# Flamingo gated layer on one core: VectorE takes a share of the first quantisations, smaller first context loads, tiles 1 and 2 loaded early, a shorter LayerNorm chain

## The chip, the cores and the metric

The kernel runs on one core of one Trainium2 chip. The metric is device time in microseconds (us) of one execution, lower is better; the time of a kernel is the median over several executions. The profile is one further execution, recorded by the hardware.

## The reference

Inputs are tokens `x` [2, 1024, 2048] and a context `cx` [2, 2048, 2048], both f32. What is computed:

```
def fake_quant(x, s, z):                    # s, z: one number each
    return (clip(round(x / s + z), 0, 255) - z) * s

x = x + tanh(g_xattn) * (fake_quant(layernorm(x)) @ fake_quant(ctx))     # per batch, 1024x2048 @ 2048x2048
y = layernorm(x)
logits = y @ route_w.T                      # 8 experts, the best one is taken
h = y @ A.T                                 # 8 experts of rank 16
x = x + tanh(g_ffn) * ((one_hot(best) * best_logit * h) @ Bw)
```

The quantised numbers are integers of at most 8 bits, so the kernel holds them as f16 with the middle (128) taken off, multiplies those, and puts scale and zero points back with a row sum and a column sum.

## The kernel before

**Tiling.** The 2048 tokens are 16 tiles `t` of 128 rows (0 to 7 are batch 0, 8 to 15 batch 1). The context of a batch is four strips `s` of 512 columns; a strip has 16 blocks of 128 rows and is loaded in four pieces `q` of 1 MB (four blocks each). I number the pieces of batch 0 by `4 s + q`: pieces 0 to 3 are strip 0, 4 to 7 strip 1, and so on to 15.

**Work of a context piece** (`strip`): SP's queue loads it into a staging buffer `st` (four of them for batch 0), ScalarE scales, shifts and rounds it into int16 (`scale`, L429), VectorE clamps it at 255, takes 128 off and turns it into f16 (`clamp`, L436). The strip `q` is then the moving operand of the matmuls. Column sums `cs` come from 16 matmuls with ones (strip 0, L454) or from VectorE additions and one matmul (L465 to L470, L480), and ScalarE writes them to `corr` (L487).

**Work of a token tile** (`tokens`): load, mean and variance (by VectorE with bn_stats, L530 to L539, for tiles in STATV, otherwise by two ScalarE passes, L545 and L554), `pow` on GpSimd (L575), a chain of 128x1 operations on VectorE (`scale`, L566 to L571), quantisation on ScalarE (`quant`, L589), clamp on VectorE (L595), turning by 16 TensorE transposes (`pq`, L613) and two copies (L496) into `q1t`, or by a DMA transpose (tiles in TURN), and a row sum (L628 on VectorE for tiles in SUMV, L630 on ScalarE).

**Products** (`group`): for each tile and strip 16 matmuls (`mm`, L657) accumulate in one of four PSUM banks; VectorE adds the bank to `x` (L686), then row and column corrections (L691); tiles in LATE have the correction added first (L669) and need one operation per strip (L678). **The second half** (`ffn`): x is turned (TensorE `px` L775, or VectorE and DMA, `turned` and `across`, for tiles in MOVE), multiplied by `war` (`hl`, L757 and L781), the expert is picked on VectorE (L830 to L839), the result is turned (`pw`, `wht`), multiplied by `wb` (`po`, L864), added (L872) and stored.

**Order.** Nothing runs in a loop's order. Every piece of work is a task with an engine, an assumed cost and a rank; `Plan.walk` simulates the engines and gives each engine a fixed instruction order, which the hardware then follows strictly: an instruction that waits holds everything behind it on its engine. Ranks come from the tables CTX, LEAD, XLEAD, XL0, AFTER, SUM and COR. `sets` lists tiles that go through a strip together: tiles 0, 1, 2 share each strip, so TensorE has 3 x 16 matmuls for each strip that it is given.

In the order of before, the first matmul group is strip 1 of tile 0, and the pieces of strips 0 and 1 are loaded and quantised mixed (4, 5, 0, 6, 1, 7, 2, 3), with x of tile 3 loaded ahead of x of tile 2.

Of the kernel before, what the change touches and what calls it, by code (L numbers as in the profile page):

```python
# [9 lines left out]
F32 = mybir.dt.float32  # L10
# [146 lines left out]
def flamingo_gated_kernel(  # L157
# [112 lines left out]
    def gates():  # L270

        nc.vector.tensor_scalar(zm1, z1, MID, None, ALU.subtract)
        nc.vector.tensor_scalar(zm2, z2, MID, None, ALU.subtract)
        nc.vector.tensor_scalar(c, th[:, 0:1], s1, s2, ALU.mult, ALU.mult)
        nc.vector.tensor_scalar(cd1, zm1, c, -1.0, ALU.mult, ALU.mult)
        nc.vector.tensor_scalar(cd2, zm2, c, -1.0, ALU.mult, ALU.mult)
        nc.vector.tensor_scalar(ckd, cd1, zm2, -float(D), ALU.mult, ALU.mult)
# [3 lines left out]

    sets = [[0, 1, 2], [3], [4], [5, 6], [7], [8, 9]] + [[t] for t in range(10, NT)]
    groups = [(t, s) for tiles in sets for s in range(NN) for t in tiles]
# [10 lines left out]

    LATE = {4, 5, 6, 7, 14}
    STATV = {0, 1, 2, 5, 15}
    SUMV = {0, 2, 5, 6, 8, 14, 15}
    COPYV = {0, 1, 2, 4, 5, 7, 9, 12, 14}
    ONES = {0}
    SUM = [-1, 8.5, 0.5, 0.5, -1, 5.5, -1, 2.5, 5.5, 2.5, -1, 3.5, 5.5, 2.5, 0.5, 8.5]  # L300
    LEAD = [4, 4, 2, 8, 6, 3, 5, 14, 5, 8, 8, 12, 7, 7, 3, 14]
    XLEAD = [4, 4, 4, 4, 2, 1, 1, 4, 10, 6, 2, 1, 0, 1, 2, 2]
    XL0 = {0: -101, 1: -2.3, 2: 1.8, 3: -0.3}
    AFTER = [1.2, 4.2, 0.3, 3.2, 0.7, 0.7, 5.2, 3.2, 0.7, 0.7, 4.2, 6.2, 4.2, 2.2, 4.2, 3.2]
    CTX = [2, 6, 5, 4, 5, 4, 3, 3]
    COR = [7.5, 1.5, 1.5, 1.5, -0.5, 2.5, 2.5, 0.5]
    SLACK = 4.0
    VIA = {0, 1, 2, 3, 4, 5, 6, 8, 9, 10, 12}
    TWO = {1, 3, 5, 6, 9, 10, 11, 12, 13, 14}
    XL = {14, 15}  # L310
    SP, ACT, DVE, PE, POOL = "SP", "ACT", "DVE", "PE", "POOL"
    add = plan.add
# [15 lines left out]
    def spread(i, j, rank, needs):  # L328

        bc = buf("cs", f"bc{i}", [P, NC], F32)  # L330
        m = add(
            PE, 0.3, rank,
            lambda: nc.tensor.matmul(bc.ap()[:, : j - i], dmean[:1, :], row[:, i:j], start=True, stop=True),
            needs + [t_one], [bc],
        )

        def out():
            nc.vector.tensor_scalar(raw[:, i:j], bc.ap()[:, : j - i], float(D), None, ALU.mult)
            if i == 0:
                nc.vector.reciprocal(rs1, s1)  # L340
                nc.vector.reciprocal(rs2, s2)

        return add(DVE, 0.6, rank + 48, out, [m], [bc])

# [16 lines left out]
    )  # L361
    t_sc = add(DVE, 1.2, 0.5, gates, needs=[t_th, t_rs])

# [46 lines left out]
    def strip(b, s):  # L410
# [5 lines left out]
        for q in range(NQ):  # L416
            st = flat(f"st{b}", f"st_{b}_{s}_{q}", F32, D)
            rank = i - CTX[b * NN + s] + q * len(tiles) / NQ

            def load(q=q, st=st):  # L420
                rows = cx[b, q * QK * P : (q + 1) * QK * P, ts(s, NC)]
                nc.sync.dma_start(  # L422
                    st.ap().rearrange("p (k n) -> p k n", k=QK),
                    rows.rearrange("(k p) n -> p k n", p=P),
                )

            def scale(q=q, st=st):
                part = qb.ap()[:, ts(q, QK), :]
                nc.scalar.activation(  # L429
                    part.bitcast(I16), st.ap().rearrange("p (k n) -> p k n", k=QK), AF.Relu,  # L430
                    bias=z2, scale=rs2,
                )

            def clamp(q=q):
                part = qb.ap()[:, ts(q, QK), :]
                nc.vector.tensor_scalar(part, part.bitcast(I16), QMAX, MID, ALU.min, ALU.subtract)  # L436

            a = t_ctx[b, s, q] = add(
                SP, 0.5, rank, load, [t_ctx[0, NN - 1, NQ - 1]] if b else [], [st],
                nbytes=4 * P * QK * NC,  # L440
            )
            d = add(ACT, 2.12, rank, scale, [a, t_rs], [st, qb])
            parts.append(add(DVE, 0.7, rank, clamp, [d], [qb]))
        t_q2[b, s] = parts
# [3 lines left out]
        if b * NN + s in ONES:  # L448
            m = None
            for q in range(NQ):  # L450
# [6 lines left out]

                m = add(PE, 0.216 * QK, rank, sums, [parts[q], t_set] + ([m] if m else []), [cs, qb])
        else:
# [38 lines left out]
    def tokens(t):  # L498
# [4 lines left out]
        xb[t] = xx = buf("xl" if t in XL else "x", f"x_{t}", [P, D], F32)  # L503
        pieces = NN if early else 1
        w = D // pieces
        loads = []
        for i in range(pieces):
            loads.append(
                add(
                    ACT if i % 2 else SP, 0.5, XL0.get(t, rank - XLEAD[t]),  # L510
                    lambda i=i: (nc.scalar if i % 2 else nc.sync).dma_start(  # L511
                        xx.ap()[:, ts(i, w)], x[b, ts(m, P), ts(i, w)]
# [5 lines left out]
        qb = flat("half", f"q1_{t}", F16, D)  # L518
        mine = small.tile([P, 28], F32, name=f"mine_{t}")
        mv, wk, acc_sums[t], fs_[t], top_[t] = (  # L520
            mine[:, i:j] for i, j in ((0, 4), (4, 12), (12, 16), (16, 24), (24, 28))
        )
        y, u, v, a, nb, rw, r, ve = (wk[:, i : i + 1] for i in range(8))
        mean, var, nmean, ssum = (mv[:, i : i + 1] for i in range(4))
        if t in STATV:
# [10 lines left out]
            def variance():  # L536
                nc.vector.bn_aggr(mv[:, :2], bn.ap())
                nc.vector.tensor_scalar(ve, var, EPS, None, ALU.add)
                nc.vector.tensor_scalar(nmean, mean, -1.0, None, ALU.mult)  # L539

            ag = add(DVE, 0.6, rank, variance, stats, [bn])
        else:
# [7 lines left out]
                lambda: nc.vector.tensor_scalar(nmean, ssum, -1.0 / D, None, ALU.mult), [d],  # L550
            )
            d = add(
                ACT, 2.3, rank,
# [10 lines left out]
        def scale():  # L564

            nc.vector.tensor_scalar(u, ve, y, None, ALU.mult)  # L566
            nc.vector.scalar_tensor_tensor(v, u, -0.5, y, ALU.mult, ALU.mult)
            nc.vector.scalar_tensor_tensor(u, v, 1.5, y, ALU.add, ALU.mult)

            nc.vector.tensor_scalar(a, u, rs1, None, ALU.mult)  # L570
            nc.vector.scalar_tensor_tensor(nb, nmean, a, z1, ALU.mult, ALU.add)  # L571

        pw = add(
            POOL, 0.3, rank,
            lambda: nc.gpsimd.tensor_tensor(y, ve, mhalf, ALU.pow), [ag, t_set],  # L575
        )
        ts_ = add(DVE, 1.2, rank, scale, [pw, t_rs])
        if t == 0:
            t_sc.needs.append(ts_)
        q1t[t] = qt = buf("q1t", f"q1t_{t}", [P, KC, P], F16)  # L580
        H = 2 if early else 1
        hw = D // H
# [3 lines left out]
        for h in range(H):  # L586
# [9 lines left out]

            d = add(ACT, 2.1 / H, rank, quant, [ts_] + loads, [xx, qb])
            clamps.append(add(DVE, 0.7 / H, rank, clamp, [d], [qb]))
            t_read.setdefault(t, []).append(d)
# [48 lines left out]
    def group(t, s):  # L648
# [5 lines left out]
        for k in range(KC):  # L654
# [4 lines left out]
                ),  # L659
                [t_q2[b, s][k // QK], t_q1t[t][k // 8]] + ([p] if p else []), [acc, qt, qb],  # L660
            )
# [282 lines left out]
```

## Time and profile before

| | us |
|---|---|
| runs | 397.11, 401.61, 399.99: median 399.99 |
| the profiled execution | 396.57 |
| its span on the core | 394.7 |
| TensorE busy, as recorded | 375.0 (95%) |
| VectorE busy | 300.7 (76%) |
| ScalarE busy | 241.4 (61%) |
| granted TensorE clock | 0.993 |

The page divides the span into 40 slices, each 9.9 us; a digit is the busy share in tenths:

```profile
PE   6686999999999999999999999999999999999894
PEld 5433455658644464645765654444644655666571
DVE  4776988996985859778678679899688787676543
```

TensorE's row is below 9 in the first four slices and again in the second to last. In the first of these the core mostly waits for data; what each engine does there is seen in the timeline and in windows of 10 us.

### The profile page before, as it was taken

Reading aid. Unit: us, or ns where it says so; the run is one execution under the profiler, and the core shown is the slowest. Engines: PE = TensorE matmul, PEld = TensorE weight load, DVE = VectorE, ACT = ScalarE, POOL = GpSimd, SP = SyncE. Lnnn points to the kernel's source line nnn. Section 1 sums busy time; section 2 is a strip of 40 time slices with the busy share of each in tenths; the row PEclk is TensorE's granted clock in tenths of the full one; section 3 lists DMA queues with packets and bytes.
Section 4 is the critical chain, followed back from the end, with each engine's and each line's share of the span. In section 5 each row is a group of like instructions: output and inputs, shape, how many; then the busy total and the mean of one; then the engine's idle time right before and its main releaser. Section 6 shows DMA issues by size and latency. Waiting matters only on the chain.

```text
span 394.7 us, 5336 instructions
## 1 busy us (share of the span) xinstructions
PE 375.0 (95%) x1969; PEld 216.8 (55%) x1969; DVE 300.7 (76%) x711; ACT 241.4 (61%) x225; POOL 23.2 (6%) x52
## 2 busy tenths in 40 slices
PE   6686999999999999999999999999999999999894
PEld 5433455658644464645765654444644655666571
DVE  4776988996985859778678679899688787676543
ACT  2998998759424680897897995939846220422330
POOL 3000000010010100010001100101000000000000
PEclk9899999999999999999999999999999999999998
DMA  7999999411469728789687978667447557766405
GB/s 272 394 398 387 387 366 405 167 31 24 118 254 338 206 44 237 293 269 372 224 248 274 343 193 319 256 198 160 78 151 204 165 176 208 219 171 208 139 18 213
DMA packets 50018, 90.07 MB, mean 228 GB/s; under 512 B 21192, under 2 KB 23240, under 8 KB 45256
## 3 DMA queue, kind: packets, MB, share of 16 engines
q1 hardware_dynamic: 45172, 69.80, 54.4%
q0 software_dynamic: 2224, 15.73, 10.0%
q10 hardware_dynamic: 2596, 4.20, 4.4%
q8 instruction: 15, 0.25, 0.2%
q14 instruction: 11, 0.09, 0.1%
HBM read 58.79 MB, written 23.07 MB: 207 GB/s over the span
## 4 chain that ended last, share of the span: by engine, by line
PE 74%; DMA 16%; SPq 3%; ACT 2%; DVE 2%; ACTq 1%; issue 1%
PE mm L657 45%; PE po L864 11%; PE hl L781 7%; PE hl L757 6%; DMA st<-in_ctx_dram 5%; DMA across<-away 4%; DMA across<-turned 4%; PE px L775 3%; DMA away<-turned 3%; ACT turned L753 1%; SPq L422 1%; SPq L731 1%; ACTq L731 1%; PE pq L613 1%; SPq L511 1%; DMA x<-in_x_dram 1%
## 5 line engine op out<-in xcount | busy, mean ns | idle before, releaser
L657 PE MATMUL mm<-q,q1t 128*128 128x512 f16 x1024 | 234.6, 381 | 6.1 <-DVE q L436 3.4
L657 PEld LDWEIGHTS <-q1t 128*128 128x128 f16 x1024 | 100.3, 98 | 126.1 <-issue 16.8
L429 ACT ACTIVATE q<-st,raw,rs 128x2048 int16<-128x2048 f32 x32 | 66.4, 2090 | 14.4 <-PE mm L657 10.0
L872 DVE SCALAR_TENSOR_TENSOR x<-po,th,x 128x512 f32<-128x512 f32 x64 | 47.6, 750 | 22.7 <-PE po L864 19.8
L864 PE MATMUL po<-wb,wht 128*128 128x512 f32 x128 | 60.7, 595 | 1.6 <-ACT wht L857 1.6
L589 ACT ACTIVATE q<-x,mine 128x2048 int16<-128x2048 f32 (+1 forms) x17 | 33.8, 1991 | 12.1 <-DVE mine L571 12.0
L819 ACT ACTIVATE junk<-x,mine 128x2048 f16<-128x2048 f32 x16 | 32.0, 2002 | 10.2 <-DVE mine L807 10.1
L757 PEld LDWEIGHTS hl<-war,turned 128*128 128x128 f32 x288 | 34.6, 190 | 3.8 <-ACT turned L753 2.4
L757 PE MATMUL hl<-war,turned 128*128 128x136 f32 x288 | 35.3, 280 | 0.6 <-ACT turned L753 0.6
L857 ACT COPY wht<-pw 128x128 f32<-128x128 f32 x16 | 4.2, 265 | 51.4 <-PE pw L851 44.4
L686 DVE SCALAR_TENSOR_TENSOR x<-mm,sc,x 128x512 f32<-128x512 f32 x44 | 32.1, 743 | 4.6 <-PE mm L657 4.5
L864 PEld LDWEIGHTS po<-wb,wht 128*128 128x128 f32 x128 | 23.1, 190 | 21.1 <-issue 14.4
L691 DVE SCALAR_TENSOR_TENSOR x<-x,mine,corr 128x512 f32<-128x512 f32 x44 | 32.1, 748 | 1.0 <-ACT corr L487 0.4
L753 ACT COPY turned<-across 128x1024 f32<-128x1024 f32 x18 | 17.9, 1042 | 21.3 <-DMA across<-turned 10.8
L781 PEld LDWEIGHTS hl<-war,xt 128*128 128x128 f32 x224 | 28.1, 190 | 2.8 <-issue 1.7
L781 PE MATMUL hl<-war,xt 128*128 128x136 f32 x224 | 29.2, 279 | 0.0
L554 ACT ACTIVATE q<-x,mine 128x2048 f16<-128x2048 f32 x11 | 22.0, 2002 | 8.8 <-DVE mine L550 8.8
L436 DVE TENSOR_SCALAR q<-q 128x2048 f16<-128x2048 int16 x32 | 21.9, 689 | 5.2 <-ACT q L429 5.0
L713 DVE STREAM_TRANSPOSE turned<-x 128x512 f32<-128x512 f32 x36 | 23.4, 687 | 0.1
L678 DVE SCALAR_TENSOR_TENSOR x<-mm,sc,x 128x512 f32<-128x512 f32 x20 | 14.8, 747 | 8.3 <-PE mm L657 8.1
L545 ACT ACTIVATE q<-x 128x2048 f16<-128x2048 f32 x11 | 21.0, 1906 | 0.0
L575 POOL TENSOR_TENSOR mine<-mine,mhalf 128x1 f32<-128x1 f32 x16 | 11.8, 739 | 152.9 <-DVE mine L561 123.5
(89 smaller groups left out, 306.9 us busy)
## 6 DMA issues: line engine op xcount, KB each, us to landing
st<-in_ctx_dram SPq DMA_DIRECT2D x32, 1024.0 KB, 11.1
x<-in_x_dram SPq DMA_DIRECT2D x15, 1024.0 KB, 9.7
out_dram<-x POOLq DMA_DIRECT2D x15, 1024.0 KB, 5.4
away<-turned SPq DMA_DIRECT2D x6, 1024.0 KB, 3.9
across<-away SPq DMA_DIRECT2D x16, 256.0 KB, 5.9
across<-away ACTq DMA_DIRECT2D x8, 256.0 KB, 6.1
across<-turned SPq DMA_DIRECT2D x24, 64.0 KB, 2.1
across<-turned ACTq DMA_DIRECT2D x24, 64.0 KB, 2.3
```

What stands on the lines that cost most here:

```text
L429: nc.scalar.activation(part.bitcast(I16), st.ap().rearrange("p (k n) -> p k n", k=QK), AF.Relu, bias=z2, scale=rs2,)
L554: lambda: nc.scalar.activation(qb.ap(), xx.ap(), AF.Square, bias=nmean, accum_out=var),
L589: nc.scalar.activation(qb.ap()[:, ts(h, hw)].bitcast(I16), xx.ap()[:, ts(h, hw)], AF.Relu, bias=nb, scale=a)
L657: lambda k=k: nc.tensor.matmul(acc.ap(), qt.ap()[:, k, :], qb.ap()[:, k, :], start=(k == 0), stop=(k == KC - 1)),
L686: lambda: nc.vector.scalar_tensor_tensor(xs(), acc.ap(), c, xs(), ALU.mult, ALU.add),
L691: lambda: nc.vector.scalar_tensor_tensor(xs(), xs(), rs_[t], corr[:, ts(s, NC)], ALU.add, ALU.add, accum_out=ss),
L713: nc.vector.transpose(turned.ap().rearrange("p (g k i) -> p k g i", i=BLK, k=KC)[:, ts(n, BPC)], xx.ap()[:, ts(n, NC)].rearrange("p (k g j ...
L757: nc.tensor.matmul(hl.ap()[:, : ER + E], turned.ap()[:, ts(k, P)], war[:, k, :], start=(k == 0), stop=(k == KC - 1),)
L781: nc.tensor.matmul(hl.ap()[:, : ER + E], xt.ap()[:, ts(k, P)], war[:, k, :], start=(k == 0), stop=(k == KC - 1),)
L819: lambda: nc.scalar.activation(junk.ap(), xx.ap(), AF.Square, bias=nm, accum_out=sq),
L864: lambda n=n, po=po: nc.tensor.matmul(po.ap(), wht.ap(), wb[:, ts(n, NC)], start=True, stop=True),
L872: nc.vector.scalar_tensor_tensor(xs, po.ap(), gf, xs, ALU.mult, ALU.add)
```

## The change

The change touches four things and the tables of the plan.

1. **Quantisation on VectorE.** A context piece whose number `2 key + h` is in `VQ` is scaled and shifted by VectorE itself (`scale_v`: f32 in, int16 out, with 128 already taken off) and clamped between -128 and 127 (`clamp_v`). By the table these are the first half of piece 0, pieces 1 and 2, the second half of piece 4, and pieces 7 and 10. The second halves of tiles 0 and 2 (SPLIT) are quantised by VectorE in the same way. 
2. **512 KB loads.** Pieces 0, 3, 4 and 5 (FINE) are loaded, scaled and clamped in halves, and each matmul waits for the part that holds its block.
3. **x loaded early and in pieces.** Tile 1 in four pieces and tile 2 in two, all on SP's queue, ahead of the context pieces 0 and 1.
4. **LayerNorm chain.** Five 128x1 operations after `pow` become four (five for SPLIT tiles), and the negated mean no longer stands ahead of `pow`.

Tables: tiles 5, 6, 7 share strips (before: 5 and 6, then 7); statistics of tile 1 go to ScalarE, of tiles 3 and 13 to VectorE; the row sums of tiles 0 and 2 and the second `q1t` copies of tiles 0, 1, 2 go to ScalarE; tile 14 leaves LATE; VIA and TWO change only for tiles that they don't concern (0, 1, 2, 5, 6 and 15 are not in MOVE), so the way in which tiles are turned stays. The order that results: SP loads x of tile 0, x of tile 1 (4 parts), piece 0 (2), x of tile 2 (2), pieces 1, 2, 3 (2), x of tile 3, then pieces 4 (2), 5 (2), 6, 10, 9, 7, 8, 11, 12, 13, 14, the weights, 15. TensorE finishes strip 0 for three tiles, then strip 1 block by block for the three tiles in turn, then strips 2 and 3. The number of TensorE instructions of each kind is unchanged. SP issues 8 more load DMAs in the opening (tile 1 three more, tile 2 one, pieces 0, 3, 4, 5 one each).

```diff
-    sets = [[0, 1, 2], [3], [4], [5, 6], [7], [8, 9]] + [[t] for t in range(10, NT)]
+    sets = [[0, 1, 2], [3], [4], [5, 6, 7], [8, 9]] + [[t] for t in range(10, NT)]
...
-    LATE = {4, 5, 6, 7, 14}
-    STATV = {0, 1, 2, 5, 15}
-    SUMV = {0, 2, 5, 6, 8, 14, 15}
-    COPYV = {0, 1, 2, 4, 5, 7, 9, 12, 14}
+    LATE = {4, 5, 6, 7}
+    STATV = {0, 2, 3, 5, 13, 15}
+    SUMV = {5, 6, 8, 14, 15}
+    COPYV = {4, 5, 7, 9, 12, 14}
...
-    CTX = [2, 6, 5, 4, 5, 4, 3, 3]
-    COR = [7.5, 1.5, 1.5, 1.5, -0.5, 2.5, 2.5, 0.5]
+    CTX = [3, 1, 3, 4, 5, 4, 3, 2]
+    COR = [1.5, 3.5, 0.5, 0.5, -0.5, 2.5, 2.5, 0.5]
...
+    PIECES = {0: 4, 1: 4, 2: 2, 3: 1}
+    SPLIT = {0, 2}
+    FINE = {0, 3, 4, 5}
+    VQ = {0, 2, 3, 4, 9, 13, 14, 17, 20, 21, 41}
+    CQ = {4: -1.8, 5: -1.1, 0: -1.1, 11: -1.0, 9: -0.2, 3: -0.1, 7: -0.6, 8: 1.1, 2: 0.2, 6: -0.9, 10: -1.5, 1: 0.7}
...
-            rank = i - CTX[b * NN + s] + q * len(tiles) / NQ
+            key = (b * NN + s) * NQ + q
+            H = 2 if key in FINE else 1
+            n = QK // H
+            for h in range(H):
+                rank = i - CTX[b * NN + s] + (q + h / H) * len(tiles) / NQ + CQ.get(key, 0)
+                k = q * QK + h * n
...
+                def scale_v(k=k, h=h, n=n, st=st):
+                    part = qb.ap()[:, k : k + n, :]
+                    nc.vector.tensor_scalar(
+                        part.bitcast(I16), st.ap().rearrange("p (k n) -> p k n", k=QK)[:, ts(h, n)],
+                        rs2, zm2, ALU.mult, ALU.add,
+                    )
+
+                def clamp_v(k=k, n=n):
+                    part = qb.ap()[:, k : k + n, :]
+                    nc.vector.tensor_scalar(
+                        part, part.bitcast(I16), -MID, QMAX - MID, ALU.max, ALU.min
+                    )
...
-                nc.vector.tensor_scalar(nmean, mean, -1.0, None, ALU.mult)
-
-            ag = add(DVE, 0.6, rank, variance, stats, [bn])
+
+            ag = add(DVE, 0.42, rank, variance, stats, [bn])
+            t_nm = add(
+                DVE, 0.15, rank,
+                lambda: nc.vector.tensor_scalar(nmean, mean, -1.0, None, ALU.mult), [ag],
+            )
...
-            nc.vector.tensor_scalar(u, ve, y, None, ALU.mult)
-            nc.vector.scalar_tensor_tensor(v, u, -0.5, y, ALU.mult, ALU.mult)
-            nc.vector.scalar_tensor_tensor(u, v, 1.5, y, ALU.add, ALU.mult)
-
-            nc.vector.tensor_scalar(a, u, rs1, None, ALU.mult)
+            nc.vector.scalar_tensor_tensor(u, ve, y, y, ALU.mult, ALU.mult)
+            nc.vector.tensor_scalar(v, u, -0.5, 1.5, ALU.mult, ALU.add)
+            nc.vector.tensor_scalar(a, v, y, rs1, ALU.mult, ALU.mult)
+
             nc.vector.scalar_tensor_tensor(nb, nmean, a, z1, ALU.mult, ALU.add)
+            if t in SPLIT:
+                nc.vector.scalar_tensor_tensor(nv, nmean, a, zm1, ALU.mult, ALU.add)
...
+            def quant_v(h=h):
+                nc.vector.tensor_scalar(
+                    qb.ap()[:, ts(h, hw)].bitcast(I16), xx.ap()[:, ts(h, hw)], a, nv, ALU.mult, ALU.add
+                )
...
+            on_v = h == 1 and t in SPLIT
+            d = add(
+                DVE if on_v else ACT, (1.32 if on_v else 2.1) / H, rank,
+                quant_v if on_v else quant, [ts_] + loads, [xx, qb],
+            )
...
-                [t_q2[b, s][k // QK], t_q1t[t][k // 8]] + ([p] if p else []), [acc, qt, qb],
+                [t_q2[b, s][k], t_q1t[t][k // 8]] + ([p] if p else []), [acc, qt, qb],
```

## The prediction

> **What bounds the kernel now.** I read the windows of 10 us first. TensorE's busy column can't be trusted in the opening; the instruction count beside it can.
>
> ```profile
> 10.00:20.00 10.00, 6.77 (x37) 4.63 (x37) 7.68 (x21) 9.20 (x7) 0.55 (x1) 0.86 1.04 394
> 20.00:30.00 10.00, 8.38 (x47) 3.83 (x46) 7.79 (x20) 10.00 (x8) 0.55 (x1) 0.97 1.02 396
> 30.00:40.00 10.00, 6.93 (x42) 3.37 (x42) 7.10 (x12) 8.58 (x6) 0.00 (x0) 1.00 1.05 387
> 40.00:50.00 10.00, 10.00 (x49) 4.49 (x47) 9.64 (x18) 10.00 (x7) 0.80 (x1) 1.00 1.05 387
> ```
>
> Columns are PE, PEld, DVE, ACT, POOL, clock, DMA share, GB/s. From 10 to 40 us ScalarE is nearly full and TensorE thin; the windows from 40 to 330 us all have TensorE at 9.6 or more. The chain of waits, in order of time, says where the dense part starts and its pace:
>
> ```profile
> 38.77 1.89 PE mm L657 x8
> 40.66 0.86 PE cs L454 x4
> 41.52 15.54 PE mm L657 x72
> 57.06 0.89 PE pq L613 x16
> ```
>
> A dense matmul takes 15.54/72 = 0.216 us, a transpose 0.89/16 = 0.056. In TensorE's order 56 `mm`, 8 `cs` and 48 `pq` stand ahead of 40.66 us: 64 x 0.216 + 48 x 0.056 = 16.5 us of work. **So 24.2 us of the first 40.7 are start-up idleness**, and as TensorE never catches up afterwards, every microsecond taken from it should shorten the run. Who holds it back? TensorE's waits name VectorE's clamp and ScalarE's copy, and the timeline shows what feeds them:
>
> ```profile
> 9.41 2.10 ACT L429 ACTIVATE q<-st,raw,rs 128x2048 int16<-128x2048 f32 x1 [1.35 <-DMA st<-in_ctx_dram]
> ...
> 24.97 0.69 DVE L530 BATCH_NORM_STATS2 bn<-x 128x6 f32<-128x512 f32 x1 [0.72 <-DMA x<-in_x_dram]
> ...
> 35.62 4.07 ACT L429 ACTIVATE q<-st,raw,rs 128x2048 int16<-128x2048 f32 x2
> ...
> 39.88 0.69 DVE L436 TENSOR_SCALAR q<-q 128x2048 f16<-128x2048 int16 x1
> ```
>
> ScalarE ends the last piece of strip 0 at 39.7 us, having worked since 9.41 on 8 pieces (16.7 us), tile quantisation (6.5), statistics and row sum (4.2), copies (2.0). The loads were earlier: the second MB is in at 9.41 and the eighth (x of tile 2) at 24.97, 2.59 us per MB, so MB n arrives at about T(n) = 9.41 + 2.59 (n - 2). The opening is bound by ScalarE's share of the quantisation and by the mixed strips.
>
> **What the Trainium skill says.** "VectorE: DVE Perf Modes", Mode 2×_2P and Side-by-side: a one-source operation with all operands in SBUF runs two f32 elements per cycle; for 2048 elements about 2293 ns at 1x, 1224 at 2x, 693 at 4x. The trace agrees on 4x (L436, 689) and on 2x of another form (L465, f16 addition, 1218); no run shows f32 to int16. "Perfetto Trace Analysis", Identifying the Most-Contended Engine: matmul busy time misleads. It does here: 42 instructions fill "6.93" us. "DMA: Bandwidth & Descriptors", Issuing engines are not separate DMA queues: all queues share 16 engines. The trace agrees: 387 to 396 GB/s in all these windows. So order can be bought, bandwidth can't.
>
> **The change, part by part.**
>
> *VectorE quantisation.* Price: 1.25 us for 2048 elements (the 2x figure plus 0.03 for two scalars per partition), 0.70 for 1024; bounds 1.22 and 2.30 (1x). Nothing makes it quicker than 2x, so a gain is excluded. ScalarE loses 4 pieces and 4 half-size operations: 4 x 2.09 + 4 x 1.1 = 12.8 us. VectorE gains 4 x 1.25 + 4 x 0.70 = 7.8; clamps cost what they did. The row sums of tiles 0 and 2 and three copies go back to ScalarE: +2 x 2.1 + 3 x 0.99 = 7.2, VectorE -2 x 2.28 - 3 x 0.68 = -6.6; tiles 1 and 3 swap the engines of their statistics (4.3 on ScalarE, 2.7 on VectorE each). ScalarE's total falls by only 5.6; what changes is *when* strip 0 is complete.
>
> I lay out the opening with durations of the trace and the new orders. x of tile 0 is in as before, its chain ends at 9.3. ScalarE stands first on tile 1's statistics (x of tile 1 is MB 2, 9.4), then quantises tile 0's first half 11.4 to 12.6; VectorE, having done the second half at 10.1, waits in order at tile 1's mean until 11.5, which is new, with tile 0's clamp and piece 0 behind it. Transposes of tile 0 start at 13.1 (before 13.5), the copy ends at 16.9, the first `mm` runs there (before 17.6). Piece 1 (T(5) = 17.2) is ready on VectorE at 19.3, piece 2 (T(6) = 19.8) at 22.1. ScalarE from 9.41: 2.1 + 1.2 + 2.2 + 1.15 + 0.99, a wait to 17.05 for tile 1's chain, then 2.08 + 0.99 + 2.1 + 1.15 + 2 x 0.99 + 1.15 + 0.99 + 1.15 = 28.6 at the last half of piece 3, and 29.4 at tile 2's last copy. TensorE: 14 `mm` of tile 2 from 29.4 to 32.4, 6 more, 4 `cs`: strip 0 done for three tiles at **34.6**. Work by then is 48 `mm`, 16 `cs`, 48 `pq` = 16.5 us: idleness 18.1.
>
> *Strip 1* is fed ahead of need (pieces 4 and 5 by 33.2, piece 6 by 37.7) but for piece 7, which SP loads after pieces 10 and 9: T(14) = 40.5. VectorE's queue there (evacuations, corrections, piece 10, clamp of tile 3) lets it start at 43.2; its clamp stands behind the clamp of piece 9, which waits for ScalarE at 43.7; ready 45.6. TensorE needs it at 44.3: 1.3 us lost. Strip 2 starts after the first bank is emptied, 49.4 against 49.6: 0.1. Idleness 18.1 + 1.4 = 19.5, against 24.2: **4.7 us gained**. Of all VectorE items here 5 f32 operations lie ahead of TensorE's need, so the 1x price takes 3 to 4 of the 4.7 away.
>
> *Smaller and earlier loads.* Eight more DMAs on SP at 0.4 to 0.5 us each, some 3.6 us; 256 KB per 0.43 us still outruns 1 MB per 2.59, so transfers hide them; taken as 0, bounds 0 and 1. That tile 1 gets in ahead is in the layout. What pays for it: piece 15 behind the weights at 65 us; TensorE needs it near 69.
>
> *LayerNorm chain.* Tiles 0 to 2: 1.11 us before (8.38 to 9.49), about 0.8 after, and 0.1 for the mean taken from ahead of `pow`. In tile 0 it hides behind ScalarE's statistics of tile 1; in tile 1 it is the 17.05 above; from tile 3 on the dense TensorE covers it.
>
> *Middle and end.* TensorE's instructions are the same in number, and dense; 5, 6, 7 sharing strips frees batch 0's strips earlier; tile 13's statistics and tile 14 without LATE give VectorE 2.4 + 0.6 us, beside dense matmuls. After the last `mm` `hl` of tile 14 is no longer to do (3.7 us), but stands ahead of it instead. The waits after it (`pw` 1.5, `po` on `wht` 1.6 in all) keep their order. I take 0 with ±1.5.
>
> **Sum.** Span 394.7 - 4.7 = 390.0, profiled execution 396.57 - 4.7 = 391.9. The runs' median, 399.99, is 3.4 above that of the profile, and they scatter by 4.5; I keep the offset: 395.2.
>
> **Rivals.**
> A. *VectorE is the bound instead* (f32 to int16 at 1x, or its in-order waits longer). For: it is 77% busy in this stage and gets waits it had not. Against: the 4x row agrees with the skill. Time: 4.7 - 3.7 = 1 gained, 399.
> B. *Given back later*: TensorE comes 4.7 us early to a product that a DMA ends (`turned` to `across` to `hl`: the chain has 10.93 us of `away` and 7.07 of `across`) and waits there. For: the chain runs through those transfers. Against: each shifts with TensorE that feeds it; dense windows on both sides. 1.5 gained, 398.5.
> C. *Slower*: a loop at the hand-over from strip 2 to 3. The bank of tile 1 is emptied on VectorE behind four corrections, which wait for ScalarE's `corr`, which stands behind piece 14, loaded into a buffer that ScalarE must free. I find bank and need at 65.5 and 65.7: no slack. Each microsecond that piece 14 is late counts whole; from 9 us on the kernel is slower by over 1%: piece 14 at 66 rather than 57, 404.5. For: SP's queue is strict, with four buffers. Against: loads ran at 387 GB/s throughout.
> D. *Hardly any effect*, if ScalarE's pieces were only shifted: the trace excludes it, strip 0 is no longer mixed with strip 1.
>
> **Chances.** A measurement of this kernel tells about 1% (4 us) from no change. Forecast 0.62, A 0.17, B 0.11, C 0.08, D 0.02. The forecast's gain, 4.7 with 1.5 for the end and the scatter of a median, is above 4 us in three of four cases and else within 1% (0.47 and 0.15); A and B, with gains of 1 to 1.5, pass 4 us by scatter alone in a third (0.10), fall within in most and below in one of ten (0.03); C is slower. Faster 0.57, same 0.32, slower 0.11. The range reaches from 389 (no loss at piece 7, end improved by 1.5, a median 3 us nearer to the profile) to 401.5 (A and B with half the runs' scatter).
>
> **What would show it.** Right: dense TensorE from 34 to 36 us with strip 0 done; f32 to int16 of 128x2048 on VectorE at 1.2 to 1.3 us; a short wait at piece 7 near 45; dense windows after, and the same waits in the last 30 us. Wrong: VectorE's f32 row near 2.3; the first `mm` after 18 us; a TensorE wait over 2 us after 50 us.

## The result, and the profile after

| | before | after |
|---|---|---|
| runs of one comparison, median (range), us | 398.29 (397.11 to 401.61), 6 runs | 393.65 (392.77 to 395.18), 6 runs |
| ratio of the times, 95% interval | | 0.9874 (0.9829 to 0.9919) |
| the profiled execution, us | 396.57 | 394.16 |
| its span, us | 394.7 | 392.4 |
| busy: TensorE, VectorE, ScalarE, us | 375.0, 300.7, 241.4 | 374.7, 305.1, 233.0 |

The changed kernel is 4.6 us faster by the medians (1.3%), and 2.4 us in the two profiled executions. 395.2 was predicted, in a range of 389.0 to 401.5. The slices of the page for TensorE and VectorE, after, to be set against those of before:

```profile
PE   4689999999999999999999999999999999999994
DVE  3699999997977398794699659999779777676553
```

The first digit of TensorE is lower than before (4, before 6), the fourth is higher (9, before 6): the first products start later, and then they run nearly without gaps. Near the end the slice below 9 was the third from last in the kernel before (8), and not the second to last; it is now 9. The windows of 10 us (columns as in the prediction: PE, PEld, DVE, ACT, POOL, clock, DMA share, GB/s):

```profile
10.00:20.00 10.00, 6.43 (x39) 5.31 (x39) 6.62 (x19) 7.15 (x7) 0.63 (x2) 0.87 0.96 345
20.00:30.00 10.00, 8.97 (x51) 4.32 (x51) 9.39 (x25) 9.42 (x9) 1.81 (x1) 0.79 1.04 396
30.00:40.00 10.00, 10.00 (x54) 4.74 (x53) 8.61 (x23) 10.00 (x10) 0.89 (x1) 1.00 1.05 387
40.00:50.00 10.00, 9.78 (x60) 5.00 (x59) 9.81 (x16) 9.90 (x8) 0.00 (x0) 1.00 1.05 387
```

TensorE is dense from 31 us, before from 40. But in the window from 10 to 20 us there is less of what feeds it: VectorE 6.62 us (before 7.68), ScalarE 7.15 (before 9.20), DMA 345 GB/s (before 394). That is where a part of the gain was lost. The chain of waits for the opening says what was late:

```profile
1.18 5.85 DMA x<-in_x_dram
7.05 0.33 SPq L539
...
9.65 11.37 DMA st<-in_ctx_dram
21.02 0.03 issue
21.05 1.36 DVE q L450
...
38.20 7.77 PE mm L704 x36
...
47.53 15.12 PE mm L704 x69
```

A piece of tile 0's `x`, issued at 1.18, lands only at 7.03. SP, which had issued three of the four parts of tile 1, issues the fourth after that, then piece 0, tile 2 and piece 1, which VectorE takes at 21.05. Strip 0 is done for three tiles at 38.20.

**The idleness, counted as in the prediction.** At 47.53, 84 `mm`, 16 `cs`, 64 `pq` and 4 `px` are done: 100 x 0.2157 + 64 x 0.0557 + 0.44 = 25.6 us of work. So 21.9 us of the first 47.5 were idle, before 24.2. In this pair the difference, 2.3 us, is the whole difference of the spans (394.7 and 392.4): the span less this idleness, called the rest below, is 370.5 us in both. (That it is the same to 0.1 us is chance, as e11 shows.) TensorE's waits, with total, times and longest:

```profile
PE mm L704 <- ACT q1t L524: 2.7, 2, 2.5
PE mm L704 <- DVE q L446: 1.4, 1, 1.4
PE pw L898 <- DVE wh L886: 1.4, 1, 1.4
...
PE pq L660 <- DVE q L629: 0.5, 1, 0.5
PE po L911 <- ACT wht L904: 0.4, 1, 0.4
```

Before, `mm` waited 3.4 us in five places for VectorE's clamp (`PE mm L657 <- DVE q L436: 3.4, 5, 1.0`); now once for 1.4. `po` on `wht` fell from 1.6 to 0.4, and `hl` on `turned` rose from 0.6 to 1.1. No wait over 1.4 us lies after the opening.

### The profile page after: what moved, and what is told of

It reads as the page before. It is cut to its first block, busy times and chain, and to the rows that moved or that the text cites. A ratio compares the mean times of both kernels' runs of the same rounds, so it can differ in the third digit from the quotient of the medians.

```text
span 392.4 us, 5340 instructions
## 1 busy us (share of the span) xinstructions
PE 374.7 (96%) x1969; PEld 216.5 (55%) x1969; DVE 305.1 (78%) x711; ACT 233.0 (59%) x225; POOL 23.6 (6%) x52
## 4 chain that ended last, share of the span: by engine, by line
PE 75%; DMA 13%; DVE 6%; ACT 2%; SPq 1%; issue 1%; ACTq 0%
PE mm L704 45%; PE po L911 12%; PE hl L804 8%; PE hl L828 6%; DMA across<-away 4%; DMA st<-in_ctx_dram 3%; DMA away<-turned 3%; PE px L822 3%; DMA across<-turned 2%; DMA x<-in_x_dram 1%; PE pq L660 1%; ACT turned L800 1%; DVE turned L760 1%; DVE x L733 1%; DVE q L450 1%
## 5 line engine op out<-in xcount | busy, mean ns | idle before, releaser
L439 ACT ACTIVATE q<-st,raw,rs 128x2048 int16<-128x2048 f32 (+1 forms) x30 | 57.3, 1919 | 13.3 <-PE mm L704 9.0
L866 ACT ACTIVATE junk<-x,mine 128x2048 f16<-128x2048 f32 x16 | 32.1, 2005 | 21.3 <-DVE mine L854 21.2
L733 DVE SCALAR_TENSOR_TENSOR x<-mm,sc,x 128x512 f32<-128x512 f32 x48 | 35.2, 744 | 10.2 <-PE mm L704 10.1
L623 ACT ACTIVATE q<-x,mine 128x2048 int16<-128x2048 f32 (+1 forms) x16 | 31.7, 1984 | 9.9 <-DVE mine L603 7.1
L804 PEld LDWEIGHTS hl<-war,turned 128*128 128x128 f32 x288 | 34.6, 190 | 5.0 <-ACT turned L800 2.8
L738 DVE SCALAR_TENSOR_TENSOR x<-x,mine,corr 128x512 f32<-128x512 f32 x48 | 35.2, 746 | 1.6 <-ACT corr L515 0.8
L587 ACT ACTIVATE q<-x,mine 128x2048 f16<-128x2048 f32 x10 | 20.0, 1997 | 8.4 <-DVE mine L582 8.4
L836 ACT COPY xt<-px 128x512 f32<-128x512 f32 x28 | 15.7, 583 | 10.7 <-PE px L822 10.7
L559 DVE BATCH_NORM_STATS2 bn<-x 128x6 f32<-128x512 f32 x24 | 15.3, 682 | 8.2 <-DMA x<-in_x_dram 8.2
L932 POOL DMA_DIRECT2D out_dram<-x x15 | 8.7, 583 | 204.5 <-DVE x L919 156.8
L677 ACT ACTIVATE q<-q 128x2048 f16<-128x2048 f16 x11 | 20.9, 1904 | 0.0
```

Of the source, the lines that this page charges most:

```text
L439: nc.scalar.activation(part.bitcast(I16), st.ap().rearrange("p (k n) -> p k n", k=QK)[:, ts(h, n)], AF.Relu, bias=z2, scale=rs2,)
L623: nc.scalar.activation(qb.ap()[:, ts(h, hw)].bitcast(I16), xx.ap()[:, ts(h, hw)], AF.Relu, bias=nb, scale=a)
L733: lambda: nc.vector.scalar_tensor_tensor(xs(), acc.ap(), c, xs(), ALU.mult, ALU.add),
L738: lambda: nc.vector.scalar_tensor_tensor(xs(), xs(), rs_[t], corr[:, ts(s, NC)], ALU.add, ALU.add, accum_out=ss),
L804: nc.tensor.matmul(hl.ap()[:, : ER + E], turned.ap()[:, ts(k, P)], war[:, k, :], start=(k == 0), stop=(k == KC - 1),)
L866: lambda: nc.scalar.activation(junk.ap(), xx.ap(), AF.Square, bias=nm, accum_out=sq),
```

## The experiments

**The theory** after this reading: the gain is VectorE's share, which completes strip 0 early, and it is cut short by late loads: tile 1 and tile 2 in small pieces arrive later than the bytes ahead of them need. **The rivals:** the loss is only one unlucky execution; the halves of the context pieces cost it; the chain costs it; or VectorE's in-order waits do, whatever the loads.

In the table, "tile 1 in" is the start of ScalarE's first pass over tile 1 (L577, waiting for the load), "tile 2 in" VectorE's first `bn_stats` of tile 2 (in brackets where it wasn't the load that ended the wait), "dense" the start of the run of 69 `mm`, idle that time less 25.6 us; the last columns are the profiled span, and span less idle.

| run | tile 1 in | tile 2 in | dense | idle | span | rest |
|---|---|---|---|---|---|---|
| after | 11.22 | 17.01 | 47.53 | 21.9 | 392.4 | 370.5 |
| e1 same again | 10.60 | 15.49 | 46.06 | 20.5 | 391.0 | 370.5 |
| e3 context whole | 11.28 | (15.27) | 46.65 | 21.1 | 392.4 | 371.3 |
| e6 old chain | 11.83 | (15.68) | 46.79 | 21.2 | 391.0 | 369.8 |
| e2 x whole | 9.34 | 14.89 | 45.03 | 19.4 | 389.1 | 369.7 |
| e12 x whole again | 9.17 | 15.02 | 45.16 | 19.6 | 389.0 | 369.4 |
| e10 whole, tiny loads | 10.08 | 16.12 | 46.27 | 20.7 | 390.4 | 369.7 |
| e9 order by hand | 10.45 | (17.64) | 46.48 | 20.9 | 392.4 | 371.5 |

**e1, the changed kernel unaltered.**

> The changed kernel once more, nothing edited, for a second trace of its opening. Theory (the eight load DMAs that were added slow the start): x of tile 0 is whole at about 7.0 us again (the three later bn_stats start at 7.0), strip 0's column sums end near 38 us, idleness up to the 47.5 us mark near 22. Rival (the slow start was chance of one execution): bn_stats at about 5.3 as in the kernel before, strip 0 done near 35 to 36 us, span near 391.

393.12 us, ratio 0.9858 (0.9816 to 0.9900). Its opening is 1.5 us shorter than in the first profile, with tile 2 in 1.5 sooner, and its rest is the same. The three later `bn_stats` of tile 0 start at 6.31, between the 7.0 of the theory and the 5.3 of the rival. So the opening varies from run to run with the landing of the loads; the first pair of profiles shows a gain of 2.3 us in it, this one 3.7.

**e2, x of tiles 1 and 2 in one load each.**

```diff
-                    ),
+                    ) if t not in (1, 2) else (nc.sync.dma_start(xx.ap(), x[b, ts(m, P), :]) if i == 0 else None),
```

The first task loads the whole tile, the others nothing.

> x of tiles 1 and 2 each in one 1 MB load, at the place of the first part; all else in the same order on every engine. Theory (small loads of x are slow, and hold SP's queue): tile 1's first ScalarE pass starts near 9.4 us instead of 11.2, piece 1 is on VectorE near 18 instead of 21.05, strip 0 done 2 to 3.5 us earlier (35 to 36), time 2 us lower than the changed kernel (ratio to the kernel before about 0.982). Rival (small loads cost nothing, chance): the opening and the time within 0.5 us of the changed kernel.

391.12 us, ratio 0.9824 (0.9777 to 0.9872). Tile 1 is in 1.3 to 1.9 us sooner than in pieces (9.34 against 11.22 and 10.60), and the idleness falls to 19.4.

**e12, the same once more.**

> x of tiles 1 and 2 in one load each, a second time and in more rounds. If whole loads bring what they seemed to bring (391.1 against 393.1 and 393.7 for pieces), tile 1 is in before 10.5 us, the idleness of the opening is 19.4 within 1, and the ratio to the kernel before is at or under 0.984. If that was the luck of one chip and one trace, tile 1 comes as with pieces, near 11, and the ratio is as in the changed kernel, 0.986 to 0.988.

391.30 us, ratio 0.9828 (0.9784 to 0.9873): it held. The timeline of e12 (start, length, engine, line, operation, tiles, and in brackets the idle time before and what ended it):

```profile
9.17 1.91 ACT L577 ACTIVATE q<-x 128x2048 f16<-128x2048 f32 x1 [0.93 <-DMA x<-in_x_dram]
...
15.02 1.29 DVE L559 BATCH_NORM_STATS2 bn<-x 128x6 f32<-128x512 f32 x2 [1.91 <-DMA x<-in_x_dram]
...
18.52 2.09 ACT L623 ACTIVATE q<-x,mine 128x2048 int16<-128x2048 f32 x1 [2.20 <-DVE mine L603]
```

And the same places in the changed kernel's timeline:

```profile
11.22 1.91 ACT L577 ACTIVATE q<-x 128x2048 f16<-128x2048 f32 x1 [1.44 <-DMA x<-in_x_dram]
...
17.01 1.29 DVE L559 BATCH_NORM_STATS2 bn<-x 128x6 f32<-128x512 f32 x2 [1.86 <-DMA x<-in_x_dram]
...
20.58 2.09 ACT L623 ACTIVATE q<-x,mine 128x2048 int16<-128x2048 f32 x1 [2.21 <-DVE mine L603]
```

Read across: 2.05, 1.99 and 2.06 us apart, and the dense run starts 2.37 apart (47.53 and 45.16). The lateness at tiles 1 and 2 is handed through to the end of the opening nearly whole. In the five runs of one order where tile 2 was waited for, dense less tile 2 is 30.1 to 30.6; this load sets the opening there. The chain of e12 runs through it (5.75 to 14.99). The chain of the first trace, shown above, runs through piece 1 instead, because with `x` in pieces piece 1 comes late too, and VectorE waits once more for it, 0.23 us in the first trace and in e1: hence 30.5 and 30.6 in these two, and 30.1 in the others.

The granted clock is not the cause of this difference. In windows of 2 us from 18 to 24 us it was 0.50, 0.50 and 0.50 in the first trace and 0.69, 0.50 and 0.95 in e12, but in the first trace TensorE waited for VectorE again after that, at 28.50 (0.2 us). In e3 and e6, where tile 2 wasn't waited for, it may have a share: there the clock was 0.50 from 16 to 24 us, four `mm` took 1.91 us (at 21.88 in e3 and 22.42 in e6; 1.03 for the next four), and TensorE waited for no clamp after its first `mm`. Their idleness is not the loads' alone.

With 1 MB loads the arrivals follow the prediction's T(n): tile 2 is the fourth MB, T(4) = 14.6, seen 14.9 and 15.0. In pieces, its first half, 3.5 MB (T = 13.3), came at 15.5 and 17.0.

**e3, the context pieces in one load each.**

```diff
-                def load(k=k, h=h, n=n, st=st):
+                def load(k=k, h=h, n=n, st=st, q=q):
+                    if h:
+                        return
+                    n = QK
+                    k = q * QK
...
-                        st.ap().rearrange("p (k n) -> p k n", k=QK)[:, ts(h, n)],
+                        st.ap().rearrange("p (k n) -> p k n", k=QK),
```

> Pieces 0, 3, 4 and 5 of the context in one 1 MB load each, quantised in halves as before, all orders kept. Theory (what hurts is the small loads ahead of the first context, so x): within 0.7 us of the changed kernel. Rival (every 512 KB load costs its own share): strip 0 done 1 us or more earlier, time lower by that. Third case (halves are worth something, as piece 0's first half can be quantised sooner): 0.3 to 1 us slower.

394.31 us, ratio 0.9885 (0.9841 to 0.9929), idleness 21.1: no different from the changed kernel. The halves of 512 KB are not the cause. The run shows more. SP's queue in the changed kernel, and then here (start, length until the last of six was issued: two parts of tile 0, four of tile 1):

```profile
1.39 5.99 SPq L539 DMA_DIRECT2D x<-in_x_dram  x6
```

```profile
1.39 4.83 SPq L543 DMA_DIRECT2D x<-in_x_dram  x6
```

Here SP had all parts of tile 1 issued by 6.22, in the first trace by 7.38; tile 1 is in at 11.28 and 11.22. In e6, whose loads are those of the changed kernel, they were issued by 6.09, and tile 1 is in at 11.83. So it isn't SP's being held to 7.05, in the chain of the first trace, that makes tile 1 late. The transfers are slower: from 6 to 8 us the DMA engines of e6 were as busy as those of e12 (share 1.01 and 0.99) and moved 214 GB/s against 402.

**e6, the old LayerNorm chain**, with the negated mean ahead of `pow` again.

```diff
-            nc.vector.scalar_tensor_tensor(u, ve, y, y, ALU.mult, ALU.mult)
-            nc.vector.tensor_scalar(v, u, -0.5, 1.5, ALU.mult, ALU.add)
-            nc.vector.tensor_scalar(a, v, y, rs1, ALU.mult, ALU.mult)
+            nc.vector.tensor_scalar(u, ve, y, None, ALU.mult)
+            nc.vector.scalar_tensor_tensor(v, u, -0.5, y, ALU.mult, ALU.mult)
+            nc.vector.scalar_tensor_tensor(u, v, 1.5, y, ALU.add, ALU.mult)
+            nc.vector.tensor_scalar(a, u, rs1, None, ALU.mult)
```

> The LayerNorm chain of the kernel before (five operations after pow, six in tiles 0 and 2, the negated mean ahead of pow), everything else changed and in the same order. Theory: 0.2 to 0.35 us later per tile of the opening, on the path in tile 1 and partly in tile 2: 0.3 to 0.6 us of idleness more, time within 0.8 us of the changed kernel's 393. Rival (the chain matters more, as VectorE is full): 1.5 us or more.

393.60 us, ratio 0.9889 (0.9846 to 0.9932). In the time the chain can't be told from nothing here. Its length can: tile 1's takes 1.08 us (18.25 to 19.33), with the new one 0.96 (19.53 to 20.49 in the first trace).

**e4, no quantisation on VectorE, in the order of the changed kernel.** The operations of `VQ` and SPLIT run on ScalarE and are clamped as the others are.

```diff
-                    scale_v if on_v else scale, [a, t_rs], [st, qb],
+                    scale, [a, t_rs], [st, qb],
...
-                quant_v if on_v else quant, [ts_] + loads, [xx, qb],
+                quant, [ts_] + loads, [xx, qb],
```

> All quantisation on ScalarE, at the same places of the global order (the plan still counts it on VectorE); the values are the same, the clamps are those of the kernel before. Theory (VectorE's share is what lets strip 0 be done early): ScalarE gets 4 x 2.09 + 4 x 1.2 = 13 us more, nearly all of it ahead of tile 3, strip 0 done 6 to 8 us later (44 to 46), time 5 to 8 us above the changed kernel, so 0 to 3 above the kernel before. Rival (the new order of the strips alone brings the gain): time within 1.5 us of the changed kernel.

407.15 us, ratio 1.0205 (1.0128 to 1.0282): 13.5 us lost against the changed kernel, more than I had expected. Its dense run starts at 57.43, with idleness 31.9; the rest is 2.7 longer, and 1.5 of that is in the 69 `mm` (16.63 against 15.12), at the start of which the granted clock was 0.50 (54 to 58 us). The largest of its waits on TensorE:

```profile
PE mm L704 <- ACT q1t L524: 6.0, 2, 3.3
PE pq L660 <- DVE q L629: 4.9, 3, 2.7
```

So the share is what the new order lives on: the eight operations are 4 x 2.09 + 4 x 1.24 = 13.3 us on ScalarE, and about as much is lost.

**e5, no share, and the plan made anew for it** (`on_v = False` in both places, so that the planner knows).

> All quantisation on ScalarE as in e4, but the plan knows it and makes its own order; loads, strips and tables as in the changed kernel. Theory (VectorE's share is needed for strip 0 to be early, the order alone does not bring it): 3 to 7 us above the changed kernel's 393, idleness of the opening 25 to 28. Rival (e4's loss came from an order that did not fit, the strip order alone brings the gain): within 1.5 us of 393.

413.27 us, ratio 1.0393 (1.0342 to 1.0444), worse still. Losses now lie late too: `hl` waits 5.2 us for `turned`, `po` 3.0 for `wht`. A new plan isn't a better one; changes of cost move instructions through the whole run. From here on I distrusted experiments that change what the planner sees.

**e7, x of tiles 1 and 2 in pieces by rows instead of columns**: four pieces of 32 rows and two of 64, each row whole.

```diff
+                    ) if t not in (1, 2) else nc.sync.dma_start(
+                        xx.ap()[ts(i, P // pieces), :], x[b, m * P + i * (P // pieces) : m * P + (i + 1) * (P // pieces), :]
                     ),
```

> x of tiles 1 and 2 in as many loads of as many bytes as in the changed kernel, but each load takes whole 8 KB rows of 32 (64) partitions instead of 2 KB (4 KB) of all rows. If the number of loads is what costs (SP held at its place in line until an earlier load lands): as the changed kernel, x of tile 2 in near 15.5 to 17 us, time 393. If the short rows cost: as e2, 391. If few partitions at a time are slow: above 393.

398.15 us, ratio 0.9991 (0.9968 to 1.0014); tile 2 is in at 22.99. Windows of 2 us of this run:

```profile
8.00:10.00 2.00, 0.42 (x3) 0.45 (x3) 1.30 (x3) 0.00 (x0) 0.00 (x0) 1.00 0.94 202
10.00:12.00 2.00, 2.00 (x10) 1.98 (x11) 1.70 (x14) 0.20 (x1) 0.56 (x1) 1.00 0.97 203
```

The DMA engines are full (share 0.94 and 0.97) and move 202 GB/s, half of the 390 of the whole loads. The Trainium skill has this, "SBUF — State Buffer", Door 1: The DMA port swizzle: partitions 0 to 31 and 0 to 63 reach only half of the ports, and 189 and 196 GB/s were measured there at 1 MiB. The trace agrees. So e7 tests another thing than I meant by it, and says nothing on short rows.

**e10, whole loads with tiny ones behind them**: tiles 1 and 2 in one load each, then three and one loads of 64 bytes into memory that nothing reads.

```diff
-                    ),
+                    ) if t not in (1, 2) else nc.sync.dma_start(*((xx.ap(), x[b, ts(m, P), :]) if i == 0 else (tiny[i][0:1, :], x[b, m * P : m * P + 1, 0:16]))),
```

> x of tiles 1 and 2 in one load each, followed by three and one loads of 64 bytes that nothing uses, so that as many loads stand in SP's queue as in the changed kernel, with the bytes in whole loads. If the number of loads and their places in line cost (SP waits for the landing of an earlier one), the idleness is as in the changed kernel, 20.5 to 22, and the time 393 to 394. If the small transfers themselves cost, it is as with whole loads, near 19.5, and 391.

394.46 us (392.17 to 396.06), ratio 0.9896 (0.9850 to 0.9941). Tile 1 in at 10.08 lies between whole loads in e2 and e12 (9.34 and 9.17; 10.45 in e9, below) and pieces (10.60 to 11.83). The idleness, 20.7, is within what pieces gave (20.5 to 21.9), and the time is no better than theirs, which is what was expected if the places in line cost. The chains of this run and of e12 have the load of tile 2, from issue:

```profile
6.82 9.27 DMA x<-in_x_dram
```

```profile
5.75 9.24 DMA x<-in_x_dram
```

It takes as long here as in e12, but is issued 1.07 us later, behind the tiny ones, and lands 1.10 later (16.09 and 14.99). That is the 1.1 us more of idleness. So places in SP's queue cost by themselves. By the rates above small transfers cost too; how the two divide in the changed kernel isn't shown.

**e8, tile 2's statistics after tile 1's chain, with whole loads**, by a dependence, so planned anew.

```diff
-                    [loads[n * pieces // NN]], [xx, bn],
+                    [loads[n * pieces // NN]] + ([ts1[0]] if t == 2 else []), [xx, bn],
```

> e2 (whole x loads), and VectorE takes the bn_stats of tile 2 only after tile 1's chain; the plan is made anew with that. In e2 the chain of tile 1 waits from about 14.5 to 17.3 us behind two pairs of bn_stats, the first of which waits for its load. Theory: the chain starts near 15.2, tile 1 is quantised 1.5 to 2 us sooner, idleness 1 to 2 us less than e2's 19.4, time 389.5 to 390.5. Rival (tile 2's own statistics are then late, or the new order runs into another wait): no better than e2's 391.

401.27 us, ratio 1.0063 (1.0040 to 1.0087). The chain of tile 1 did start at 16.15 instead of 17.34, but the new plan lost more than that in other places, `mm` waiting 2.8 and 2.0 us for VectorE and `cs` 1.6, and the rest was 375.2. A miss, and the reason for the next one.

**e9, the same by hand**, in the finished order, all other instructions left in place.

```diff
+    for task in stats_[2]:
+        order.remove(task)
+    i = order.index(ts__[1]) + 1
+    while order[i].eng != DVE:
+        i += 1
+    i += 1
+    order[i:i] = stats_[2]
```

> x of tiles 1 and 2 in one load each, and in VectorE's order by hand, nothing else planned anew: the four bn_stats of tile 2 stand behind the chain of tile 1 and the clamp of the second half of piece 0. If tile 2's statistics, waiting for their load, hold tile 1's chain, the chain starts near 15.4 us (17.3 with whole loads alone), ScalarE quantises tile 1 about 1.5 us sooner, the idleness of the opening falls from 19.4 to about 18 and the time is near 390. The rival: VectorE then does the statistics ahead of piece 1, which comes 1.3 us later, and the idleness stays at 19.4 or rises, 391 to 392.

392.80 us (391.74 to 394.22), ratio 0.9858 (0.9824 to 0.9893). Tile 1 was quantised at 17.50, 1.0 us before e12, although its load came 1.3 later. But VectorE then does all four statistics ahead of piece 1, which starts at 20.02, in e12 at 18.67. What tile 1 gains, piece 1 loses: the rival's answer. The later load makes the size of the trade uncertain.

**e11, the kernel before once more.**

> The kernel before once more, for a second trace of its opening. If the gain lies in the opening and the spread of runs elsewhere or in the loads, the idleness is 24.2 within 0.5 and the rest of the span 370.5 within 0.5. If the rest of the span moves by 2 us or more from run to run, the split between opening and rest is not to be trusted.

399.02 us, span 397.1. The opening ends where it did in the first trace, to 0.01 us (72 `mm` from 41.53, before from 41.52), so the idleness is 24.2 again. But it didn't begin so: the first `bn_stats` of tile 1 starts at 13.12 (11.86 in the first trace) and the first `mm` at 18.87 (17.61). This lateness of 1.26 us is gone at a context load that lands at 31.6 in both. The chain of the first trace, then this run's:

```profile
12.65 18.96 DMA st<-in_ctx_dram
31.64 2.10 ACT q L429
```

```profile
13.63 18.00 DMA st<-in_ctx_dram
31.65 2.10 ACT q L429
```

ScalarE waits 1.42 us for it in the first trace, 0.19 here, and from there on the openings agree. It is the sixth context load, piece 7, which belongs to strip 1. So in the kernel before, the end of the opening hangs on that landing, and a load of tile 1 that was late ahead of it cost nothing.

The rest is 2.4 us longer, which by the expectation speaks against trusting the split. The last stretch of both chains, first this run's, then the first trace's:

```profile
387.31 5.41 PE po L864 x8
```

```profile
386.63 3.71 PE po L864 x8
```

1.7 of the 2.4 us are in the last eight `po`, with a granted clock of 0.75 in the last window (0.86 in the first trace). Up to 337 us the two chains agree within 0.3 us. So the opening's count stands, but the rest of a single run is good to 2 us only.

## Why the prediction was right, and where it wasn't

| step | predicted | after | e12, whole loads |
|---|---|---|---|
| chain of tile 0 ends | 9.3 | 11.2 | 9.7 |
| ScalarE starts on tile 1 | 9.4 | 11.22 | 9.17 |
| first `mm` | 16.9 | 18.42 | 16.37 |
| tile 1 quantised from | 17.05 | 20.58 | 18.52 |
| piece 1 ready | 19.3 | 23.1 | 20.7 |
| strip 0 done for three tiles (start of the next `mm`) | 34.6 | 38.0 | 35.7 |
| loss after it | 1.4 | 0.2 | 0.2 |
| idleness | 19.5 | 21.9 | 19.6 |

- **Direction and time: right, in part by luck.** The gain by the medians of one comparison, 4.6 us, is the 4.7 predicted, and e1's comparison gives 4.75. But the prediction had all of it in the opening, and there the two traces of the changed kernel show 2.3 and 3.7. Over two traces of each kernel the opening gives 3.0 and the rest 1.2, most of it in the last eight `po` of e11, which the prediction doesn't have. The 3.4 us by which the first median of before (399.99) stood above its profile was partly the luck of three runs: over six it is 398.29. That is the rest of the way from 395.2 to 393.65.
- **Failed term: "Eight more DMAs on SP ... transfers hide them; taken as 0, bounds 0 and 1".** They weren't hidden. In the changed kernel tile 1 was 1.8 us behind the layout, the first half of tile 2 3.7 us, and strip 0 3.4 (in e1 1.2, 2.2 and 1.9). Putting the four of `x` back into whole loads takes 0.9 to 2.5 us of idleness away; the four of the context cost nothing that could be seen (e3). The upper bound, 1, was too low. The windows of 2 us from 6 to 16 us show it: 272 to 327 GB/s in the first trace of the changed kernel and 246 to 376 in e1, 378 to 451 before, and with whole loads 387 to 424 in all but one (278 and 294 from 8 to 10 us). The Trainium skill's "SBUF — State Buffer", The DMA setup-cost knee, gives a fixed part for every transfer, 224 GB/s at 256 KiB and 341 at 1 MiB for transfers one at a time; here several are in flight, so the figures are not those of this case, and the traces agree in direction only. I had compared the rate of issue with that of whole loads, and set no price on a small transfer or on a place in the queue. The "wrong" mark that I set, first `mm` after 18 us, came up in the first trace (18.42), not in e1 (17.80).
- **Tile 0, late in the first trace, is not shown to belong to that term.** Its last three `bn_stats` start at 7.06, before at 5.33. But its loads are issued ahead of every load that was added, and in e3, e4 and e6, with the same parts of tile 1 behind them, these operations start at 5.52, 5.32 and 5.38. What delayed it stays open.
- **Tile 1's chain behind tile 2's statistics.** The layout has no wait there: by T(n) the first half of tile 2 was to be in at 13.3. Even with whole loads it comes at 15, and tile 1 is quantised 1.5 us later than laid out. e9 shows that moving them only moves the loss.
- **Piece 7: mis-sized, 1.3 predicted, about 0 seen.** It was ready at 48.20 (clamp L457, 47.51 + 0.69), behind the clamp of piece 9 as laid out. TensorE came to it at 48.18, as it was late itself and had three `mm` of tile 3 to do first. e12, whose strip 0 was done at 35.7, shows no stall there either. In e12 this error (1.2 us less lost) cancels the one before (strip 0 1.1 later), so that its idleness, 19.6, comes to the 19.5 predicted: two errors, not a hit.
- **f32 to int16 on VectorE: 1.34 us for 2048 elements, 0.81 for 1024,** predicted 1.25 and 0.70, outside the 1.2 to 1.3 that I named as right, and far from 2.30:

```profile
13.66 0.81 DVE L450 TENSOR_SCALAR q<-st,rs,zm 128x1024 int16<-128x1024 f32 x1
...
24.00 1.34 DVE L450 TENSOR_SCALAR q<-st,rs,zm 128x2048 int16<-128x2048 f32 x1
```

  The second 1024 elements take 0.53 us, twice the 0.27 of the clamp (0.69 less 0.42), which the prediction had as 4x; so the 2x speed holds with int16 out, and rival A's price is out. Its other half, longer waits in VectorE's order, came in part: the wait for tile 2 above. e4 shows that this share carries the change, worth 13.5 us in its order.
- **LayerNorm chain: mis-sized.** "About 0.8 after" was predicted for the 1.11 of before; 0.96 was measured, 0.12 less than the old chain in e6. What that is worth in the time isn't shown (e6: 21.2 idle against 20.5 and 21.9).
- **Middle and end, 0 with 1.5: not contradicted.** The rest is 370.5 in both traces of the changed kernel, 370.5 and 372.9 in those of before. Rival B would have shown waits on `hl`; they grew by 0.5 us on `turned` and by 0.4 on `xt`. Rival C's hand-over from strip 2 to 3 shows no stall: TensorE has no wait of 0.2 us or more between 50 and 80 us.
- **Smaller slips of the working.** "The loads were earlier" doesn't hold for piece 7 (e11). The 42 instructions in "6.93" us are 22 `mm`, 4 `cs` and 16 `pq`, 6.5 us at the dense pace, so that the busy column misleads little in that window. ScalarE's fall of 5.6 us leaves out tile 13's statistics (4.3), with which it is 9.9; 8.4 was measured (241.4 to 233.0). 49.4 against 49.6 is 0.2, not 0.1, and 399.99 - 4.7 is 395.3.

**A faster version:** e12 (and e2), the changed kernel with `x` of tiles 1 and 2 in one load each, at 391.3 and 391.1 us against 393.1 and 393.65 of the changed kernel and 398 of before. The intervals of the ratios overlap (0.9784 to 0.9873 and 0.9829 to 0.9919), so that it beats before is shown, and that it beats the changed kernel is likely: the openings of both its traces are shorter.

**Left open:** what of the late small loads is their place in SP's queue and what the transfers themselves, in the changed kernel; why tile 0 came late in its first trace; what VectorE's share would bring in the old order of strips (e4 and e5 take it away in the new one, and no run adds it to the old); and whether `x` of tile 0, in four pieces in every kernel here, would come sooner otherwise. No run here tries these.

## What to carry to other kernels

A load that is split so that its first part can be used sooner may bring every part later: compare the arrival of the last byte that the next step needs with that of the whole load, and lay out the opening by bytes landed, not by order of issue. Where an engine takes its work strictly in order, a load that comes late is handed on to all that stands behind it: one landing set the start of the dense part here to within 0.5 us. It is handed on only until a later landing ends the wait anyway: in the kernel before, 1.26 us of lateness were gone by 31.6 us. So look for the landing that ends last, and repeat a trace before a lateness is put down to a change. When a planner makes the order, test an edit in the finished order first; the planner's answers to small changes cost 6 us (e5 against e4) and 10 us (e8 against e2) here.

## What was not expected of the hardware

- In the changed kernel a `pow` of 128x1 on GpSimd took 1.81 us beside a clamp and then an f32 operation of 128x2048 on VectorE, and ended 0.03 us after the latter; 12 of the 16 take 0.55 to 0.56, the other three 0.89 to 1.46. The Trainium skill's "SBUF — State Buffer", Who interferes with whom, says that such a VectorE mode and GpSimd shut each other out for a whole instruction; the trace agrees. Nothing waited for it.
- The last eight `po` of the same kernel took 3.71 us in one execution and 5.41 in another, with the granted clock of the last window at 0.86 and 0.75.
